# Cross attention: attention probabilities transposed by transfers of 16-bit halves instead of on TensorE

## The chip, the cores and the metric

The kernel runs on one core of one Trainium2 chip. A core has five engines that run side by side, each with its own instruction stream that it works through in order: TensorE (PE in the profile; its weight loads are PEld), VectorE (DVE), ScalarE (ACT), GpSimd (POOL) and SyncE (SP), which here issues nearly all transfers. 16 DMA engines move the data. The on-chip memory SBUF has 128 partitions; TensorE writes to a second memory, PSUM. The metric is the device time of one execution in microseconds (us), lower is better. The kernel before takes 880.24 us, the median of three runs (879.62 to 881.49).

## The reference

One layer of a perceiver in single precision. 16 batches; each has 64 latent rows `x` and a context of 512 rows, all of width 512. Three stages, each added to `x`: cross attention of the latents over context and latents, self attention with two softmaxes, and a gated feed-forward with weights and activations rounded to a 4-bit grid. The change lies in the first:

```
xn = _ln(x, g_x, b_x)                       # x: the context, (16, 512, 512)
ln = _ln(latents, g_l, b_l)                 # (16, 64, 512)
q = ln @ w_q
kv_in = jnp.concatenate([xn, ln], axis=1)   # 576 rows
k, v = jnp.split(kv_in @ w_kv, 2, axis=-1)  # 8 heads of 64
sim = jnp.einsum('bhid,bhjd->bhij', q, k)   # masked
attn = jax.nn.softmax(sim, axis=-1)
out = jnp.einsum('bhij,bhjd->bhid', attn, v)
return _ln(out.transpose(...) @ w_out, g_o, b_o)
```

So per batch and head there is a 64 x 576 matrix of probabilities. The product with `v` sums over the 576, and TensorE sums over partitions: the probabilities, which come out with the queries on the partitions, have to be transposed first.

## The kernel before

The program first works out the latents' queries, keys and values (`latents`), then the cross attention over the batches (`cross_attention`), into whose spare time on VectorE, ScalarE and GpSimd it lays the rounding of the feed-forward weights (`quant.tick()`), and then self attention and feed-forward. The order of instructions of every engine is the order of the program text; it is written out by hand, and `in_order` (L82) keeps it.

All large products are made three times (`Common.terms`, L114 to 126): both operands are split in a high and a low part, and high times high, low times high and high times low are summed, with four chunks of 128 each, so 12 matmuls of 512 columns for one product. The context comes twice: with its rows on the partitions (`nat`, 1 MB a batch, for mean and deviation, `Context.load` and `stats`) and transposed (`raw`, four chunks of 256 KB, `fetch`), which ScalarE casts to the high part (`Context.high`, L362) and VectorE or GpSimd subtracts from to get the low part (`Context.low`, L368).

The loop over the batches (L1152 and on) has in each batch b this order on TensorE, with what stands beside it:

- `keys(b, 0)`: a product for the keys of heads 0 and 1; VectorE scales it out of PSUM (L941). Then `turn(b - 1)` and `turn_latents(b - 1)`; in odd batches from 3 on also the transpose of an earlier output (`out_turn`, `ot`).
- `keys(b, 1)`, `keys(b, 2)`, `keys(b, 3)`, and between them ScalarE's casts of the next context and the loads of the one after.
- `scores(b, 0)` for the first pair of key chunks (four heads), `softmax(b, 0)`: VectorE takes the scores out of PSUM with the mask (L986), ScalarE takes the exponential (L990), into a tile `pr` of 2 x 576 columns, two buffers.
- `finish(b - 1)`: the product of the previous batch's probabilities with its values, first the latents' part (`weigh_latents`, L1039), then the context's (`weigh`, L1055), in the order r = 0 of pair 0, r = 0 of pair 1, r = 1 of pair 0, r = 1 of pair 1.
- `scores(b, 1)`, `softmax(b, 1)`.
- `values(b, 0)` to `values(b, 3)`: products for the values; ScalarE scales them out of PSUM (L954). In odd batches an output product (`po`) stands between the second and the third.
- At the end: ScalarE writes the next batch's mask (L913), SP issues the load of `nat` three batches on (`cx.load`, L314).

`turn` (L994) transposes the context's part of the probabilities of a batch: for two pairs `a`, two rows of heads `r`, four blocks `j` of 128 columns and two heads `c` one transpose of 64 x 128 on TensorE (L1004), 32 in all, into two PSUM tiles; ScalarE copies them to four tiles `prT` (L1013), which `weigh` uses as stationary operands. `turn_latents` (L1016) does the same with the 64 latent columns: two transposes, one copy to a tile `prl` (tag `two_h`, two buffers).

SP issues transfers one after the other; each first waits for the semaphore of its lane, of which there are eight, so at most eight are under way, and for the engines whose data or buffers it needs. What stands behind a waiting issue waits too.

Of the kernel before, what the change touches and what calls it, by code (L numbers as in the profile page):

```python
# [9 lines left out]
F32 = mybir.dt.float32  # L10
F32R = mybir.dt.float32r
U32 = mybir.dt.uint32
U8 = mybir.dt.uint8
AF = mybir.ActivationFunctionType
ALU = mybir.AluOpType
AX = mybir.AxisListType
# [3 lines left out]
P = 128  # L20
D = 512
KC = D // P
B = 16
S = 64
# [835 lines left out]
def cross_attention(tc, cm, sc, i, cw, cx, w1, w2, att, quant):  # L860
# [41 lines left out]
    def latents_values(b):  # L902
        if b >= B:
            return
        p, e = divmod(b, 2)
        vl = state[b]["vl"] = w2.tile([P, KC, S], F32, tag="two_l", bufs=2, name=f"vl_{b}")
        src = sc.v[p][e * S : (e + 1) * S].rearrange("p (n two d) -> p n two d", two=2, d=S)
        for h in range(2):
            nc.sync.dma_start(vl[h * S : (h + 1) * S], src[:, :, h, :])
# [22 lines left out]
    def keys(b, m):  # L932

        k = ends.pop((b, m))
        hi, lo = cx.done[b]
        cols = slice(m * P, (m + 1) * P)
        ps = cm.mm(f"pk_{b}_{m}")
        cm.product(
            ps, lambda c: (w_k[0][:, c, cols], w_k[1][:, c, cols], hi[:, c, :], lo[:, c, :]), range(KC)
        )  # L940
        nc.vector.tensor_tensor(k[:, S : S + N], ps, cx.row[b], ALU.mult)  # L941
        state[b]["k"].append(k)
# [31 lines left out]

    def softmax(b, a):
        st = state[b]
        st["pr", a] = w1.tile([P, 2, N + S], F32, tag="pr", bufs=2, name=f"pr_{b}_{a}")

        def two(t):
            return t.rearrange("p (h n) -> p h n", h=2)  # L980

        for r, ps in enumerate(st.pop(("sim", a))):
            mask = masks[b % 2][:, columns_of(r)[0]]
            pr = st["pr", a][:, r, :]
            least = cm.small.tile([P, 1], F32, tag="least", name=f"least_{b}_{a}_{r}")
            nc.vector.tensor_tensor_reduce(  # L986
                two(pr), ps[:, :, :half], two(mask), -1.0, BIG, ALU.add, ALU.min, least
            )
            t = 2 * a + r
            nc.scalar.activation(  # L990
                pr, pr, AF.Exp, bias=least, scale=-1.0, accum_out=st["tot"][:, t : t + 1]
            )

    def turn(b):  # L994

        pts = [cm.two(f"prt_{b}_{a}") for a in range(2)]
        for a, pt in enumerate(pts):
            for r in range(2):
                first = columns_of(r)[1].start
                for j in range(NJ):  # L1000
                    at = (r * NJ + j) * S
                    for c in range(2):
                        rows = slice(c * S, (c + 1) * S)
                        nc.tensor.transpose(  # L1004
                            pt[:, c, at : at + S],
                            state[b]["pr", a][rows, r, first + j * P : first + (j + 1) * P],
                            cm.ident[rows, rows],
                        )
        for a, pt in enumerate(pts):
            for r in range(2):  # L1010
                prT = w1.tile([P, NJ, P], F32, tag="prT", bufs=4, name=f"prT_{b}_{a}_{r}")
                src = pt[:, :, r * NJ * S : (r + 1) * NJ * S].rearrange("p c (j q) -> p c j q", q=S)
                nc.scalar.copy(prT.rearrange("p j (c q) -> p c j q", q=S), src)  # L1013
                state[b]["prT", a, r] = prT

    def turn_latents(b):  # L1016
        st = state[b]
        prl = w2.tile([P, 2, P], F32, tag="two_h", bufs=2, name=f"prl_{b}")
        pt = cm.ps_av.tile([P, D], F32, tag="av", name=f"prlt_{b}")[:, : 2 * P]
        pt = pt.rearrange("p (n q) -> p n q", q=P)  # L1020
        for a in range(2):
            pr = st.pop(("pr", a)).rearrange("p r t -> p (r t)")
            nc.tensor.transpose(pt[:, a, :], pr[:, N : N + P], cm.ident)
        nc.scalar.copy(prl, pt)
        st["prl"] = prl

    def weigh_latents(b):

# [123 lines left out]
    for b in range(B):  # L1152

        def tick():
            if b:
                quant.tick()

        done = (b - 3) // 2 if b >= 3 and b % 2 else None
        last = b == B - 1
        keys(b, 0)  # L1160
        if last:
            att.load("Wq")
            att.load("Wk")
        cx.high(b + 1, 0)
        if b >= 4 and b % 2 == 0:
            out_moments((b - 4) // 2)
        if b > 1:
            tick()
        if b:
            turn(b - 1)  # L1170
            turn_latents(b - 1)
        if done is not None:
            out_turn(done)
        keys(b, 1)
        cx.low(b + 1, 0)
        cx.high(b + 1, 1)
        if b > 1:
            tick()
        keys(b, 2)
        if done is not None:  # L1180
            out_low(done)
        cx.fetch(b + 2, 0)
        if b == 0:
            for k in range(KC):
                load_o(k)
        cx.flat(b + 1)
        cx.low(b + 1, 1)
        cx.high(b + 1, 2)
        tick()
        if last:  # L1190
            att.split("Wq", 0, 1)
        if b == 0:
            scores(b, 0)
            softmax(b, 0)
        keys(b, 3)
        cx.fetch(b + 2, 1)
        if b:
            scores(b, 0)
            softmax(b, 0)
        cx.low(b + 1, 2)  # L1200
        cx.high(b + 1, 3)
        if b:
            finish(b - 1)
            scores(b, 1)
            softmax(b, 1)
            around(b + 1, 2, 3)
            around(b + 2, 0, 1)
        tick()
        values(b, 0)
        cx.every(b + 1)  # L1210
        cx.low(b + 1, 3)
        cx.stats(b + 2, 0)
        tick()
        if last:
            att.split("Wq", 2, 3)
            att.load("Wv")
        if b == 0:
            scores(b, 1)
            softmax(b, 1)
            around(b + 1, 2, 3)  # L1220
            around(b + 2, 0, 1)
        values(b, 1)
        begin(b + 1)
        latents_values(b + 1)
        cx.fetch(b + 2, 2)
        cx.stats(b + 2, 1)
        tick()
        if last:
            att.norm(0)
            att.split("Wk", 0, 1)  # L1230
        tick()
        if done is not None:
            out_product(done)
        tick()
        values(b, 2)
        cx.fetch(b + 2, 3)
        cx.stats(b + 2, 2)
        tick()
        if done is not None:
            out_norm(done)  # L1240
            out_add(done)
        if b == 0:
            weight_o(0)
            weight_o(1)
        if b == 2:
            att.sa.load()
        if b == 5:
            att.sa.work()
        if last:
            att.split("Wk", 2, 3)  # L1250
            att.load("Wo")
            att.turn(0)
        values(b, 3)
        cx.stats(b + 2, 3)
        cx.spread(b + 2)
        mask(b + 1)
        if b == 0:
            weight_o(2)
            weight_o(3)
        quant.tick()  # L1260
        cx.load(b + 3)
    turn(B - 1)
# [42 lines left out]
class SelfAttention:  # L1305
# [42 lines left out]
    def turn(self, t):  # L1348
        cm, w2 = self.cm, self.w2
        pt = cm.ps_av.tile([P, D], F32, tag="av", name="zt_1") if t == 1 else cm.tr(f"zt_{t}")  # L1350
        cm.transpose_chunks(pt, self.st.pop(("z", t)), KC)
        zh = w2.tile([P, KC, P], F32R, tag="two_h", bufs=2, name=f"zh_{t}")
        zl = w2.tile([P, KC, P], F32R, tag="two_l", bufs=2, name=f"zl_{t}")
        cm.split(zh, zl, pt.rearrange("p (k n) -> p k n", n=P))
        self.st["zT", t] = zh, zl
# [299 lines left out]
class FeedForward:  # L1655
# [111 lines left out]
    def turn_h(self, s):  # L1767
        cm, w2 = self.cm, self.w2
        t, c = s
        n = CHUNKS[c][1]  # L1770
        nk = n // P
        pt = cm.tr(f"ht_{t}_{c}")
        cm.transpose_chunks(pt, self.st.pop(("h", s)), nk)
        hh = w2.tile([P, KC, P], F32R, tag="two_h", bufs=2, name=f"hh_{t}_{c}")[:, :nk, :]
        hl = w2.tile([P, KC, P], F32R, tag="two_l", bufs=2, name=f"hl_{t}_{c}")[:, :nk, :]
        src = pt[:, :n].rearrange("p (k n) -> p k n", n=P)
        if s == self.steps[-1]:
            for k in range(nk):
                cm.nc.scalar.copy(hh[:, k, :], src[:, k, :])
            cm.nc.vector.tensor_tensor(hl, src, f32(hh), ALU.subtract)  # L1780
        else:
            cm.split(hh, hl, src)
        self.st["hT", s] = hh, hl
# [171 lines left out]
```

## Time and profile before

| | |
|---|---|
| median of 3 runs | 880.24 us (879.62 to 881.49) |
| profiled execution | 881.33 us |
| span of its instructions | 879.5 us |
| TensorE busy | 871.7 us, 99% of the span |
| weight loads | 719.2 us, 82% |
| VectorE busy | 687.2 us, 78% |
| ScalarE busy | 398.8 us, 45% |
| GpSimd busy | 296.2 us, 34% |
| queue q1 (transfers of SP) | 80136 packets, 109.48 MB, 38.2% of 16 engines |
| granted TensorE clock | 1.0 throughout the cross attention |

The span is the time from the first to the last instruction of one profiled execution. "Busy" is the time in which at least one instruction of the engine ran. The chain of waits is followed back from the last instruction, at each step to what released it. A group of instructions is given by line, engine, operation, the tiles written and read, the shapes and the count, then busy us and mean ns of one, then the idle time of the engine just before them and who ended it. In a timeline x4 means four such instructions in a row, and the time is theirs together. The cross attention runs from about 92 to 560 us; batch 10 starts at 373.88, batch 11 at 401.98, batch 12 at 433.19.

### The profile page before, as it was taken

Reading aid. Unit: us, or ns where it says so; the run is one execution under the profiler, and the core shown is the slowest. Engines: PE = TensorE matmul, PEld = TensorE weight load, DVE = VectorE, ACT = ScalarE, POOL = GpSimd, SP = SyncE. Lnnn points to the kernel's source line nnn. Section 1 sums busy time; section 2 is a strip of 40 time slices with the busy share of each in tenths; the row PEclk is TensorE's granted clock in tenths of the full one; section 3 lists DMA queues with packets and bytes.
Section 4 is the critical chain, followed back from the end, with each engine's and each line's share of the span. In section 5 each row is a group of like instructions: output and inputs, shape, how many; then the busy total and the mean of one; then the engine's idle time right before and its main releaser. Section 6 shows DMA issues by size and latency. Waiting matters only on the chain.

```text
span 879.5 us, 17521 instructions
## 1 busy us (share of the span) xinstructions
PE 871.7 (99%) x6743; PEld 719.2 (82%) x6743; DVE 687.2 (78%) x1457; ACT 398.8 (45%) x787; POOL 296.2 (34%) x341
## 2 busy tenths in 40 slices
PE   8999999999999999999999999999999999999998
PEld 8988787878787888778878888888888888888887
DVE  7734457789788887787888867688998897888876
ACT  5654454544544535354445455554556233332221
POOL 2334234235353352353433622545543120111100
PEclk9999999999999999999999999999999999999999
DMA  8464554644655455435644362240008330000000
GB/s 277 167 233 169 167 163 142 201 143 141 192 164 160 138 174 168 136 111 178 183 134 149 121 198 64 82 192 1 1 3 320 136 144 13 13 13 13 13 12 25
DMA packets 80379, 111.12 MB, mean 126 GB/s; under 512 B 33176, under 2 KB 39080, under 8 KB 79016
## 3 DMA queue, kind: packets, MB, share of 16 engines
q1 hardware_dynamic: 80136, 109.48, 38.2%
q8 instruction: 53, 0.87, 0.4%
q0 software_dynamic: 160, 0.52, 0.2%
q14 instruction: 30, 0.25, 0.1%
HBM read 84.26 MB, written 25.72 MB: 125 GB/s over the span
## 4 chain that ended last, share of the span: by engine, by line
PE 93%; DVE 3%; DMA 2%; ACT 1%; POOL 1%; issue 1%; SPq 0%; ACTq 0%; DVEq 0%; POOLq 0%
PE pv L121 20%; PE pk L121 19%; PE gu L121 13%; PE dn L121 6%; PE sim L967 4%; PE av L1055 4%; PE Wv L121 3%; PE wo L121 3%; PE po L121 2%; PE Wq L121 2%; PE Wk L121 2%; PE prt L1004 2%; PE lq L121 2%; PE lk L121 2%; PE lv L121 1%; PE ht L171 1%
## 5 line engine op out<-in xcount | busy, mean ns | idle before, releaser
L121 PE MATMUL pv<-xvh,x 128*128 128x512 f32 x512 | 133.0, 394 | 0.0
L121 PE MATMUL pk<-x,xkh 128*128 128x512 f32 x512 | 128.2, 392 | 0.0
L121 PEld LDWEIGHTS pv<-xvh,x 128*128 128x128 f32 x512 | 94.8, 188 | 26.2 <-issue 7.0
L121 PEld LDWEIGHTS pk<-x,xkh 128*128 128x128 f32 x512 | 94.9, 188 | 19.5 <-issue 0.4
L990 ACT ACTIVATE pr<-pr,least 128x576 f32<-128x576 f32 x64 | 49.1, 769 | 59.7 <-DVE least L986 59.7
L941 DVE TENSOR_TENSOR k<-pk,row 128x512 f32<-128x512 f32 x64 | 43.2, 675 | 39.2 <-PE pk L121 39.0
L368 POOL TENSOR_TENSOR x<-raw,x 128x512 fp32r<-128x512 f32 x32 | 41.6, 1301 | 85.8 <-ACT x L362 80.5
L121 PE MATMUL pv<-xvl,x 128*128 128x512 f32 x256 | 68.7, 390 | 0.0
L121 PE MATMUL pk<-x,xkl 128*128 128x512 f32 x256 | 68.5, 389 | 0.0
L954 ACT ACTIVATE v<-pv,rs 128x512 f32<-128x512 f32 x64 | 43.2, 684 | 54.8 <-PE pv L121 54.3
L121 PE MATMUL gu<-uT,fx 128*128 128x512 f32 (+1 forms) x288 | 67.0, 377 | 0.2 <-DMA uT<-u_d 0.2
L121 PE MATMUL gu<-gT,fx 128*128 128x512 f32 (+1 forms) x288 | 65.8, 376 | 0.0
L121 PEld LDWEIGHTS gu<-gT,fx 128*128 128x128 f32 x288 | 52.2, 188 | 7.6 <-ACT fx L129 0.2
L121 PEld LDWEIGHTS gu<-uT,fx 128*128 128x128 f32 x288 | 51.8, 188 | 7.7 <-DMA uT<-u_d 0.5
L121 PEld LDWEIGHTS pv<-xvl,x 128*128 128x128 f32 x256 | 48.0, 188 | 10.3
L121 PEld LDWEIGHTS pk<-x,xkl 128*128 128x128 f32 x256 | 48.1, 188 | 10.2
L986 DVE CUSTOM_DVE_ANT_0 pr<-sim,mask 128x576 f32<-128x576 f32 x64 | 45.8, 753 | 5.3 <-PE sim L967 4.3
L205 ACT ACTIVATE qe_h<-qe_h,mmagic 128x512 f32<-128x512 f32 (+1 forms) x24 | 16.5, 687 | 66.7 <-DVE qe_h L202 64.6
L321 DVE BATCH_NORM_STATS2 cst<-nat 128x6 f32<-128x512 f32 x64 | 42.8, 669 | 3.7 <-DMA nat<-in_ctx_dram 3.7
L121 PE MATMUL dn<-dT,hh 128*128 128x512 f32 x170 | 42.9, 392 | 0.0
L967 PE MATMUL sim<-k,mask 64*64 64x288 f32 x512 | 40.4, 415 | 0.3 <-DMA mask<-q_d 0.3
L362 ACT CAST x<-raw 128x512 fp32r<-128x512 f32 x64 | 39.1, 631 | 0.0
(347 smaller groups left out, 1867.1 us busy)
## 6 DMA issues: line engine op xcount, KB each, us to landing
nat<-in_ctx_dram SPq DMA_DIRECT2D x16, 1024.0 KB
raw<-in_ctxT_dram SPq DMA_DIRECT2D x64, 256.0 KB
d_d<-qhl_d SPq DMA_DIRECT2D x11, 512.0 KB
row<-rs_d SPq DMA_DIRECT2D x16, 256.0 KB
g_d<-qhl_g SPq DMA_DIRECT2D x8, 512.0 KB
u_d<-qhl_u SPq DMA_DIRECT2D x8, 512.0 KB
gT<-g_d SPq DMA_DIRECT2D x4, 1024.0 KB
uT<-u_d SPq DMA_DIRECT2D x4, 1024.0 KB
```

The source lines that it names most:

```text
L121: self.nc.tensor.matmul(ps, lhsT=p[i], rhs=p[j], start=start and n == 0, stop=stop and n == last)
L205: nc.scalar.activation(e, e, AF.Relu, bias=self.mmagic, scale=MAGIC)
L321: nc.vector.bn_stats(st, self.nat[b][:, j, :])
L362: self.cm.nc.scalar.copy(self.done[b][0][:, c, :], self.raw[:, c, :])
L368: by.tensor_tensor(lo, self.raw[:, c, :], f32(hi), ALU.subtract)
L941: nc.vector.tensor_tensor(k[:, S : S + N], ps, cx.row[b], ALU.mult)
L954: nc.scalar.mul(v, ps, cx.rs[b][:, t : t + 1])
L967: nc.tensor.matmul(pss[r][c * S : (c + 1) * S, h, :half], lhsT=queries[b % 2][rows, m, :], rhs=st["k"][m][rows, at : at + half], start=Tru ...
L986: nc.vector.tensor_tensor_reduce(two(pr), ps[:, :, :half], two(mask), -1.0, BIG, ALU.add, ALU.min, least)
L990: nc.scalar.activation(pr, pr, AF.Exp, bias=least, scale=-1.0, accum_out=st["tot"][:, t : t + 1])
L1004: nc.tensor.transpose(pt[:, c, at : at + S], state[b]["pr", a][rows, r, first + j * P : first + (j + 1) * P], cm.ident[rows, rows],)
L1055: nc.tensor.matmul(st["av"][r][rows, a, :], lhsT=prT[:, j, rows], rhs=st["v"][j][:, at : at + S], start=False, stop=j == NJ - 1, skip_grou ...
```

## The change

For batches 0 to 14 the context's probabilities are no longer transposed by TensorE. Four bytes of a number are taken as two 16-bit halves:

- `halves(b, a)`: ScalarE copies the low and the high halves of a pair's probabilities into two 16-bit tiles of 2 x 512 columns (tag `two_h`, now three buffers). For pair 0 right behind the first value copy (in batch 0 behind the second), for pair 1 at the end of the batch, behind the fourth value copy and the mask.
- `send(b, a)`: SP issues for each half one transfer that transposes, 128 partitions x 1024 columns in blocks of 128 x 128, into a tile `far`, which takes a buffer of tag `pr`. For pair 0 behind the third value product, for pair 1 behind the first key product of the next batch.
- `join(b, a)`: ScalarE puts the two halves of each number together again and writes `prT`, two copies a pair. For pair 0 behind the second key product of the next batch, for pair 1 behind the third.

`turn_latents` stays on TensorE, but moves from behind the first key product of the next batch to behind the second value product of its own. Its target `prl` now shares a tile with the latents' values (`both`, tag `two_l`). The last batch keeps `turn` and `turn_latents` as they were. The tile of the probabilities is made 128 columns wider, so that a regular view `wide` reaches the context's columns of both rows.

```
@@ latents_values
-        vl = state[b]["vl"] = w2.tile([P, KC, S], F32, tag="two_l", bufs=2, name=f"vl_{b}")
+        both = w2.tile([P, 2, KC * S], F32, tag="two_l", bufs=2, name=f"lat_{b}")
+        vl = state[b]["vl"] = both[:, 0].rearrange("p (n d) -> p n d", d=S)
+        state[b]["prl"] = both[:, 1].rearrange("p (n q) -> p n q", q=P)
@@ softmax
-        st["pr", a] = w1.tile([P, 2, N + S], F32, tag="pr", bufs=2, name=f"pr_{b}_{a}")
+        wide = w1.tile([P, 2 * (N + 2 * S)], F32, tag="pr", bufs=2, name=f"pr_{b}_{a}")
+        st["wide", a] = wide.rearrange("p (r n) -> p r n", r=2)
+        st["pr", a] = wide[:, : 2 * (N + S)].rearrange("p (r n) -> p r n", r=2)
@@ new
+    def halves(b, a):
+        st = state[b]
+        src = st.pop(("wide", a))[:, :, :N].bitcast(U16).rearrange("p r (n h) -> p h r n", h=2)
+        for h in range(2):
+            half = w2.tile([P, 2, N], U16, tag="two_h", bufs=3, name=f"half_{b}_{a}_{h}")
+            nc.scalar.copy(half, src[:, h])
+            st["half", a, h] = half
+
+    def send(b, a):
+        st = state[b]
+        far = w1.tile([P, 2 * (N + 2 * S)], F32, tag="pr", bufs=2, name=f"far_{b}_{a}")
+        far = far[:, : 2 * N].bitcast(U16).rearrange("p (h n q) -> p h n q", h=2, q=P)
+        for h in range(2):
+            half = st.pop(("half", a, h)).rearrange("p r n -> p (r n)")
+            nc.sync.dma_start(far[:, h], half, transpose=True)
+        st["far", a] = far
+
+    def join(b, a):
+        far = state[b].pop(("far", a))
+        for r in range(2):
+            prT = w1.tile([P, NJ, P], F32, tag="prT", bufs=4, name=f"prT_{b}_{a}_{r}")
+            dst = prT.rearrange("p j q -> p (j q)").bitcast(U16).rearrange("p (n h) -> p n h", h=2)
+            src = far[:, :, r * NJ : (r + 1) * NJ].rearrange("p h j q -> p (j q) h")
+            nc.scalar.copy(dst, src)
+            state[b]["prT", a, r] = prT
@@ turn_latents
-        prl = w2.tile([P, 2, P], F32, tag="two_h", bufs=2, name=f"prl_{b}")
+        prl = st["prl"]
@@ the loop over the batches
         keys(b, 0)
+        if b:
+            send(b - 1, 1)
...
-        if b:
-            turn(b - 1)
-            turn_latents(b - 1)
...
         keys(b, 1)
+        if b:
+            join(b - 1, 0)
...
         keys(b, 2)
+        if b:
+            join(b - 1, 1)
...
         values(b, 0)
+        if b and not last:
+            halves(b, 0)
...
         values(b, 1)
+        if b == 0:
+            halves(b, 0)
+        if not last:
+            turn_latents(b)
...
         values(b, 2)
         cx.fetch(b + 2, 3)
+        if not last:
+            send(b, 0)
...
+        if not last:
+            halves(b, 1)
         quant.tick()
         cx.load(b + 3)
```

Outside the cross attention only the number of buffers of `two_h` changes from two to three, in `SelfAttention.turn` and `FeedForward.turn_h`.

## The prediction

> **What bounds the kernel now.** I read the page first, then the chain of waits over one batch of the cross attention, then ScalarE, the queue of SP and the DMA engines in that same batch. From the page, busy times and the chain that ended last:
>
> ```profile
> PE 871.7 (99%) x6743; PEld 719.2 (82%) x6743; DVE 687.2 (78%) x1457; ACT 398.8 (45%) x787; POOL 296.2 (34%) x341
> ...
> PE 93%; DVE 3%; DMA 2%; ACT 1%; POOL 1%; issue 1%; SPq 0%; ACTq 0%; DVEq 0%; POOLq 0%
> ```
>
> TensorE is the bound, and its instructions follow each other without gaps. So whatever is taken from it is gained, as long as nothing it waits for comes later than it comes now. The chain of waits in batch 11, which starts at 401.98 (start us, us, what):
>
> ```profile
> 401.98 2.72 PE pk L121 x12
> 404.69 1.14 PE prt L1004 x32
> 405.83 0.37 PE prlt L1023 x2
> 406.20 0.44 PE ot L171 x4
> 406.64 8.18 PE pk L121 x36
> 414.81 1.13 PE sim L967 x16
> 415.94 0.23 PE av L1039 x16
> 416.18 2.02 PE av L1055 x64
> ```
>
> The reader sees the price of `turn`: 32 transposes of probabilities, 1.14 us a batch. They lie right behind the first key product, and their results are used some 10 us later, by `av` L1055. Busy time by stage for an even and an odd batch (PE, PEld, DVE, ACT, POOL, clock, DMA share, GB/s), and for two microseconds inside the odd one:
>
> ```profile
> 373.88:401.98 28.10, 28.10 (x244) 22.51 (x243) 23.41 (x53) 13.77 (x28) 13.16 (x15) 1.00 0.49 144
> 401.98:433.19 31.21, 31.21 (x259) 25.19 (x259) 24.77 (x59) 14.55 (x31) 10.96 (x13) 1.00 0.51 161
> ...
> 406.00:408.00 2.00, 2.00 (x13) 1.75 (x12) 0.39 (x1) 1.54 (x4) 0.79 (x1) 1.00 0.94 349
> ```
>
> ScalarE and the DMA engines are half free, VectorE only a sixth. But at 406 to 408 the DMA engines are full: that is the 1 MB load of the next context (`nat`), issued as the timeline of SP shows (start, us, what):
>
> ```profile
> 403.15 0.38 SPq L314 DMA_DIRECT2D nat<-in_ctx_dram  x1
> ```
>
> **The change, part by part.** All times below, called T, count from the start of a batch.
>
> *Removed from TensorE:* `turn` of batches 0 to 14 (that of batch 15 stays): 15 x 1.14 = 17.1 us, all of it on the path.
>
> *Moved:* `turn_latents` (prlt, 0.37) goes from the next batch's start to behind the second value product. Same instructions, 0 us, but a nearer deadline: it needs the second pair's exponentials, which ended at 421.67 + 0.18, so T = 19.9, and with `turn` gone earlier at about 18.4. TensorE gets there at 10.9 + 0.44 + 1.13 + 0.23 + 2.02 + 1.13 + 5.4 = 21.3. Cover 2.9 us; 0 us.
>
> *ScalarE.* These groups give the prices (busy, mean ns), and the timeline shows that copies in a row overlap:
>
> ```profile
> L1013 ACT COPY prT<-prt 128x512 f32<-128x512 f32 x64 | 32.6, 594 | 0.0
> ...
> L1456 ACT ACTIVATE ex<-ex 128x1024 f32<-128x1024 f32 x8 | 8.5, 1062 | 22.6 <-DVE ex L1447 22.6
> ```
>
> ```profile
> 406.88 2.04 ACT L1013 COPY prT<-prt 128x512 f32<-128x512 f32 x4
> ```
>
> Four copies of 512 went, 0.51 each. Eight of 1024 elements come (four `halves`, four `join`); 1062 ns less the same overlap of some 0.1 is 0.96 each. Net 8 x 0.96 - 2.04 = 5.6 us a batch, so ScalarE is at 19.4 of about 27 in the even batch. The two copies behind the first value copy fit between it and the second (the product between them takes 2.72, the value copy 0.69, leaving 2.0 for 1.9). The join reads its two 16-bit parts alternately from places 2 KB apart; no row of this trace reads so. From below it costs as a plain copy, 0.96; from above twice that. I take the plain price, as no strided row here is dearer (the prT copies also rearrange), and keep the upper end as a rival.
>
> The Trainium skill (SBUF — State Buffer, the note on "cachelines") speaks against that price: accesses that change the 16-byte line each time pay a penalty, and the join's reads do. It gives no figure; no run here shows it yet.
>
> *The transfers.* Per batch four transposing transfers of 256 KB on the queue of SP. None is in this trace. One engine of 16 gets 64 pieces if a piece is a 256-byte source row. The trace's packets of 256 bytes took 17.8 ns on average, so t = 64 x 17.8 ns = 1.14 us a transfer. From above: if pieces were as small as what lands in one partition (16 values, 32 bytes), there would be 512 per engine at about 9.8 ns (packets of 4 bytes took 9.0, of 128 bytes 11.9), so t = 5.0 us. I take 1.14, since the source rows are 256 bytes and rows of that very size are in the trace.
>
> The rule in VectorE: DVE Perf Modes, "The three transpose paths", speaks against the whole change: it puts a 128x128 block at 1309 ns by transfer against 390 by TensorE. Eight blocks in a row at that price would be 10.5 us a transfer, and the four of a batch 42; with the 14 the engines have now that is 28 over the batch's 28, 15 x 28 = 420 us, some 1300 in all (estimates from that page). This trace shows TensorE's side far cheaper than 390 (1.14 us for 32 half blocks) and nothing of the other.
>
> *Does the second pair arrive in time?* The fourth value copy ends at T = 0.7 (402.70), the mask at 1.3, the two half copies at 2.3 and 3.25. SP can issue at 2.4 and 3.3. The `nat` load stands before them in the same queue; its packets end near T = 6.5 (408.5; the 256 KB behind it is issued later in the new order). So the transfers land at 6.5 + 2t + 0.4 = 9.2, the joins end at 10.1 and 11.1. TensorE comes to the weighing of that pair at 10.9 + 1.13 + 0.23 + 0.5 = 12.76, and to its second half at 13.76. Cover 2.6 us; it is gone at t = 2.45. The first pair has more than half a batch: no cost.
>
> *What stands behind the wait.* ScalarE comes to the second `join` at about T = 6.7 and waits 2.5 us. Behind it are a cast of the next context, the exponentials, and now and then a ScalarE step of the weight quantiser, on which VectorE waits in order, and VectorE frees the PSUM of the key products. Now such a step costs VectorE 0.3 us:
>
> ```profile
> L207 DVE SCALAR_TENSOR_TENSOR qw_g<-qe_g,qw_g 128x512 f32<-128x512 f32 (+1 forms) x12 | 8.2, 682 | 3.5 <-ACT qe_g L205 3.4
> ```
>
> From below 0 (VectorE has 28.10 - 23.41 = 4.7 us free); from above the whole 2.5 of each batch, 37 us. I take 0.5 us a batch, 7.5 us, nearer the lower end because VectorE uses the cast behind the wait only at 417.52 (T = 15.5, without `turn` about 14), after the joins have ended.
>
> *SP.* 60 more issues. An issue now takes 0.33 to 0.6 us; the longest single rows are 2.0 (with a wait in it). Four a batch: 1.5 to 8 us on a queue that is solid from 414.4 to 429.1 and then rests until 434.3. The first pair's two fall into that rest. At 0.6: 0 us. At 2.0 the second pair would land at 3.3 + 2 x 2.0 + 1 = 8.3 at the earliest, still below 9.2; the loads behind (the context's next chunk, issued at 410.73, T = 8.75) then have no rest left. So 0, and up to 1 us a batch above 2.0.
>
> *The rest:* three tiles in place of two for `two_h`, the latents' tile joined with `vl`, and `far` in the buffers of `pr`: `far` of pair 1 needs only its own half copies; the next batch's first exponentials' tile needs the joins that ended at 11.1, used at T = 13. Cover 2 us; 0. Batch 15 and all behind it are untouched.
>
> *Sum.* -17.1 + 7.5 = -9.6 us. The profiled execution took 881.33 (span 879.5 and 1.8 around it), 1.1 above the median: 881.3 - 9.6 = 871.7, and on the median 880.24 - 9.6 = 870.6. I say 871.
>
> **The rivals.**
>
> *Small pieces (slower).* If transfers move at the 32-byte price, the pair lands at 6.5 + 10 + 0.4 and the join ends at 17.9 instead of 12.76: 5.1 us late a batch, less 1.14. And the DMA engines have 20 us more beside their 0.5 x 28.1 = 14: 34 in a batch of 28, 6.5 over, 15 x 6.5 = 98 us: 979. It starts to cost at t = 2.45 and cancels the gain at 3.0. For it: no transposing row here. Against: whole 256-byte source rows. Its middle is 930.
>
> *The join at half speed (slower).* 1.82 instead of 0.96, 4 x 0.86 = 3.4 us a batch more. The joins end at 11.0 and 12.9, just in time, but ScalarE is at 23 of 27 and everything behind is late. None of it on TensorE: 871; all of it: 871 + 51 = 922. A third, since 3 us stay idle: 888. It decides above 0.65 us a batch.
>
> *SP runs out (slower or same).* Issues of 2.5 us and more delay `nat` and the context's chunks; 1 us a batch is lost: 886; at about 2 us the gain is just used up on VectorE's waits: 880.
>
> *Nothing new (hidden anyway)* is excluded for the removed part: TensorE does not wait there now.
>
> **How the numbers follow.** Forecast 0.45, with a range of its own from 863 (no wait at all) to 878. Small pieces 0.20, evenly from 880 to 980. Half-speed join 0.20. SP 0.15, half of it within 0.2%, which is about what a measurement of this kernel can tell from no change (1.8 us). Faster 0.45, same 0.08, slower 0.47. The range goes from 862 to 930, which leaves out half of the small pieces and little else.
>
> **What would show it.** No prt before batch 15; PE busy lower by 17 us; half and join copies near 1 us each (the rival: 1.8); ScalarE waiting for a transfer at the second join for about 2.5 us; av L1055's line without a wait for ScalarE; DMA share up from 0.5 to some 0.65 (0.9 and more if pieces are small); transposing issues on SP of 0.6 us (2 and more for that rival). The prediction is wrong if TensorE waits for the joins, and the size of that wait over 15 batches says by how much.

## The result, and the profile after

| | before | after |
|---|---|---|
| median | 880.2 us (879.62 to 881.49) | 886.66 us (886.17 to 887.05) |
| ratio after / before | | 1.0071 (95% interval 1.0054 to 1.0088) |
| profiled execution, span | 881.33, 879.5 | 886.17, 884.4 |

The change makes the kernel 0.7% slower; 871 was forecast, and faster. The time lies inside the range, on the other side of no change. The page of the kernel after, busy times and the chain that ended last:

```profile
PE 862.4 (98%) x6263; PEld 708.2 (80%) x6263; DVE 686.8 (78%) x1457; ACT 488.4 (55%) x847; POOL 294.7 (33%) x341
...
PE 67%; DMA 11%; DVE 11%; ACT 6%; SPq 3%; issue 2%; POOL 1%; DVEq 0%; ACTq 0%; POOLq 0%
```

TensorE's work fell, by 9.3 us in this row, not by the 17 that the prediction gives as its sign: the scores' busy time rose from 40.4 to 44.8 us and the weighing's from 33.4 to 37.0, some of it at the slow clock of the last section. And the chain, 93% TensorE before, is now only 67% TensorE: transfers and VectorE have taken a tenth each. The same from the start of batch 0 (at 81.76 before, ten us earlier than the start of the cross attention given above) to the start of batch 15, first before, then after (window, length, busy us of PE, PEld, DVE, ACT, POOL, then TensorE's clock, DMA share, GB/s):

```profile
81.76:520.42 438.66, 438.38 (x3613) 351.32 (x3612) 341.41 (x769) 209.34 (x421) 174.50 (x196) 1.00 0.51 157
```

```profile
81.79:525.86 444.07, 429.60 (x3167) 340.54 (x3166) 341.49 (x770) 295.57 (x480) 172.66 (x197) 0.99 0.72 187
```

The whole loss is in these 15 batches, 5.4 us. TensorE was idle for 0.3 us there and is now idle for 14.5; ScalarE has 86 us more, and the DMA engines went from half to 0.72 busy. Batch by batch (us from one first key product to the next):

| batch | 0 | 1 | 2 | 3 | 4 | 5 | 6 | 7 | 8 | 9 | 10 | 11 | 12 | 13 | 14 |
|---|---|---|---|---|---|---|---|---|---|---|---|---|---|---|---|
| before | 25.4 | 28.1 | 28.1 | 31.5 | 28.1 | 31.8 | 28.1 | 31.6 | 28.1 | 31.2 | 28.1 | 31.2 | 28.1 | 31.2 | 28.1 |
| after | 27.4 | 32.2 | 27.7 | 36.4 | 27.7 | 33.2 | 27.9 | 31.4 | 26.8 | 30.5 | 26.8 | 30.0 | 27.2 | 32.2 | 26.8 |

Batches 8, 10, 11 and 14 show the gain undisturbed: 1.30 us in an even batch and 1.25 in an odd one. Over 15 batches that is some 19 us. Batches 0, 1, 3, 5 and 13 are longer than before by 13.4 us together, more than the others gain (8.0). The waits of TensorE in the cross attention of the kernel after (waited for: us in total, times, longest):

```profile
PE av L1088 <- ACT prT L1047: 9.9, 5, 4.6
PE sim L970 <- DVE least L991: 2.3, 6, 0.6
PE prlt L1057 <- ACT pr L995: 2.0, 1, 2.0
```

The first row is the weighing of the second pair, which waits for the joins. The chain of waits in batch 3 says what the joins waited for (start us, us, what):

```profile
177.93 8.06 DMA far<-half
...
186.06 1.17 ACT prT L1047
187.23 0.04 issue
187.27 2.45 PE av L1088 x48
189.72 1.86 PE sim L970 x16
```

The second transposing transfer took 8.06 us from its issue to its landing. The timeline of SP there:

```profile
171.69 0.57 SPq L294 DMA_DIRECT2D g_d<-qhl_g  x1
...
175.90 0.38 SPq L315 DMA_DIRECT2D nat<-in_ctx_dram  x1
176.39 6.05 SPq L1037 DMA_TRANSPOSE far<-half  x2
```

Ahead of the pair stand a 512 KB store of the quantiser, some small loads and the 1 MB `nat`; the two issues alone hold SP for 6.05 us. The groups of copies on ScalarE and of the weighing on TensorE:

```profile
L1047 ACT COPY prT<-far 128x1024 uint16<-128x1024 uint16 x60 | 67.2, 1173 | 20.3 <-DMA far<-half 20.3
...
L1027 ACT COPY half<-pr 128x1024 uint16<-128x1024 uint16 x60 | 59.7, 1041 | 2.4 <-DMA far<-half 2.4
...
L1088 PE MATMUL av<-v,prT 128*64 128x64 f32 x1024 | 37.0, 231 | 10.0 <-ACT prT L1047 9.9
```

The copies cost little more than forecast. But ScalarE waits 20.3 us at the joins, and TensorE 9.9 us behind them. VectorE waits as well, for a cast that stands behind the joins on ScalarE:

```profile
DVE x L369 <- ACT x L363: 15.8, 5, 4.5
```

The two longest of these waits, 4.5 and 4.1 us, lie in batches 1 and 3, behind the late pair. The kernel before has no wait for this cast.

### The profile page after: what moved, and what is told of

It reads as the page before. It is cut to its first block, busy times and chain, and to the rows that moved or that the text cites. A ratio compares the mean times of both kernels' runs of the same rounds, so it can differ in the third digit from the quotient of the medians.

```text
span 884.4 us, 16760 instructions
## 1 busy us (share of the span) xinstructions
PE 862.4 (98%) x6263; PEld 708.2 (80%) x6263; DVE 686.8 (78%) x1457; ACT 488.4 (55%) x847; POOL 294.7 (33%) x341
## 4 chain that ended last, share of the span: by engine, by line
PE 67%; DMA 11%; DVE 11%; ACT 6%; SPq 3%; issue 2%; POOL 1%; DVEq 0%; ACTq 0%; POOLq 0%
PE gu L122 14%; PE pv L122 12%; PE pk L122 7%; PE dn L122 7%; DMA far<-half 4%; PE sim L970 3%; PE Wv L122 3%; PE wo L122 2%; PE Wq L122 2%; PE Wk L122 2%; PE po L122 2%; PE av L1088 2%; PE lq L122 2%; PE lk L122 2%; DMA g_d<-qhl_g 2%
## 5 line engine op out<-in xcount | busy, mean ns | idle before, releaser
L122 PE MATMUL pv<-xvh,x 128*128 128x512 f32 x512 | 135.1, 395 | 0.0
L122 PEld LDWEIGHTS pv<-xvh,x 128*128 128x128 f32 x512 | 94.2, 188 | 25.7 <-issue 7.2
L1047 ACT COPY prT<-far 128x1024 uint16<-128x1024 uint16 x60 | 67.2, 1173 | 20.3 <-DMA far<-half 20.3
L1027 ACT COPY half<-pr 128x1024 uint16<-128x1024 uint16 x60 | 59.7, 1041 | 2.4 <-DMA far<-half 2.4
L122 PEld LDWEIGHTS pv<-xvl,x 128*128 128x128 f32 x256 | 48.0, 188 | 10.5
L206 ACT ACTIVATE qe_h<-qe_h,mmagic 128x512 f32<-128x512 f32 (+1 forms) x24 | 16.5, 687 | 66.4 <-DVE qe_h L203 64.3
L970 PE MATMUL sim<-k,mask 64*64 64x288 f32 x512 | 44.8, 429 | 2.3 <-DVE least L991 2.3
L1088 PE MATMUL av<-v,prT 128*64 128x64 f32 x1024 | 37.0, 231 | 10.0 <-ACT prT L1047 9.9
```

The costliest lines, as they stand in the source:

```text
L122: self.nc.tensor.matmul(ps, lhsT=p[i], rhs=p[j], start=start and n == 0, stop=stop and n == last)
L206: nc.scalar.activation(e, e, AF.Relu, bias=self.mmagic, scale=MAGIC)
L970: nc.tensor.matmul(pss[r][c * S : (c + 1) * S, h, :half], lhsT=queries[b % 2][rows, m, :], rhs=st["k"][m][rows, at : at + half], start=Tru ...
L1027: nc.scalar.copy(half, src[:, h])
L1047: nc.scalar.copy(dst, src)
L1088: nc.tensor.matmul(st["av"][r][rows, a, :], lhsT=prT[:, j, rows], rhs=st["v"][j][:, at : at + S], start=False, stop=j == NJ - 1, skip_grou ...
```

## The experiments

Theory A: the second pair comes late because of what stands ahead of it on SP's queue. Theory B: ScalarE's eight copies a batch, in order with everything else there, are the price. Theory C: the transposing issues hold up SP, and what is behind them is late.

**Without the transfers (e2).** In `send` and `join`:

```
-            nc.sync.dma_start(far[:, h], half, transpose=True)
+            (left out; join reads the probabilities where they lie)
```

> The changed kernel without its 60 transposing transfers: the joins read the probabilities where they lie (untransposed, so the output is another), the halves are still copied and thrown away. ScalarE's eight copies a batch stay, SP's issues and the transfers go. Theory A (late arrival): all of the gain shows, 15 x 1.3 us as in the undisturbed batches: 880.2 - 19.5 = 861, no wait of TensorE over 1 us. Theory B (ScalarE's work): 880 to 887 as before. Theory C: as A, 861; A and C are told apart by the other runs.

Measured: 872.32 us (871.15 to 872.74), ratio 0.9913 (0.9897 to 0.993). So the transfers cost 14.3 us of the 886.7. But it is not 861: some 11 us go in another way, to which e13 to e17 return. Batch 7 shows where (chain of waits; it starts at 282.34):

```profile
296.56 0.68 DVE k L944
297.24 0.67 DVE pr L992
...
297.96 1.87 PE sim L970 x16
```

VectorE comes late to the keys and the scores, and the second scores on TensorE (1.13 us undisturbed) follow at its pace.

**Without the load ahead (e9).**

```
+        if 3 <= b < B:
+            self.nat[b] = self.kept          # context 2's tile, no transfer
```

> The changed kernel (886.7 us) without the 1 MB load of nat for contexts 3 to 15 (13 MB of the queue; their statistics are taken from context 2, so the output is another). All transposing transfers, their issues, the stores and all copies stay. Theory A (the second pair is late because of what stands ahead of it on the one queue): only the 512 KB store is left ahead, the pair lands before T = 9.5 in every batch, TensorE's waits for the joins go, and the kernel comes to the level of e2, 871 to 875. Theory C (the transposing transfers themselves, 1.24 us and more of SP each and 1.6 us of the engines): they are all still there, 884 to 888.

875.23 us (874.43 to 877.72), ratio 0.9942 (0.9926 to 0.9957). The 60 transposing transfers and their issues are still there; with the 13 loads out of their way 11.4 of the 14.3 us come back. TensorE's wait for the joins:

```profile
PE av L1091 <- ACT prT L1050: 1.2, 3, 0.6
```

From 9.9 us to 1.2. A shorter wait of VectorE for `nat` itself is not the reason: it is 3.4 us in the kernel after, and 4.3 here. So theory A holds, and the transfers and their issues alone (theory C) cost no more than the rest of some 3 us.

**The pair first, the load behind it (e1).**

```
             send(b - 1, 1)
+            cx.load(b + 2)
...
-        cx.load(b + 3)
```

> The 1 MB load of the next context (nat) is issued behind the second pair's two transposing transfers, not ahead of them; nothing else differs from the changed kernel (886.7 us). Theory A (the second pair arrives late because nat, and in odd batches a 512 KB store of the quantiser too, stand ahead of it in the one queue): the second pair lands some 3 us earlier, the waits of TensorE for the joins (3.68, 4.65, 0.92, 0.49 us in batches 1, 3, 13, 5) shrink to a fifth at most, and with them the slow clock behind the two long ones (2 us each): 886.7 - 8 - 4 = 875, and 868 if the small waits of VectorE go as well. Theory B (ScalarE's eight copies a batch are the price, in order with the casts and exponentials): the copies are all still there, 884 to 888. Theory C (SP is held up by each transposing issue, 1.24 us and more, and what is behind comes late): the issues are all still there, and nat now comes behind them: 885 to 892.

901.42 us (900.89 to 902.0), ratio 1.0242 (1.0227 to 1.0258): slower than any theory had it. What A said of the pair came true: the odd batches from 3 to 11 took 29.96 us, and the wait for the joins went to 2.4 us. But the even batches took up to 37.8. Their chain of waits, in batch 4:

```profile
216.04 7.17 DMA u_d<-qhl_u
...
223.31 0.10 DVE qhl_u L288
...
225.33 2.86 PE sim L970 x16
228.19 7.45 PE pv L122 x24
```

The quantiser's store now stands behind `nat`. VectorE refills the store's buffer, so it waits for its landing, and the scores wait for VectorE (20.1 us in all). The wait had been moved, not removed. A part of the 901 is the slow clock behind these waits: the mean granted clock was 0.985, against 0.996 in the kernel after, which is some 10 us of clock time over the span (an estimate from these two numbers). The run also shows an undisturbed transposing transfer, in a window in which only the pair moves:

```profile
460.40:463.10 2.70, 2.70 (x14) 2.23 (x13) 2.63 (x6) 2.52 (x3) 2.36 (x5) 1.00 1.01 191
```

All DMA engines are busy, at 191 GB/s: 256 KB in 1.37 us.

**The load behind the store too (e5), and batch 0's latents later (e6).** e5 puts `cx.load(b + 2)` ahead of `keys(b, 2)`; e6 moves `turn_latents(0)` behind `values(0, 2)` besides.

> As e1_send_first (901.4 us), but the load of nat goes one step further back, behind the quantiser's 512 KB store that follows the two transfers. In e1 the joins were on time and VectorE waited instead for that store, whose buffer it refills (TensorE waited 20.1 us for VectorE, and the even batches lost 36 us against the undisturbed 26.8). Theory A2 (what hurts is only which item stands behind the 1 MB load; an order exists in which nobody waits): the store lands some 3 us earlier, these 36 us go, and the kernel comes to 865 to 872. Theory D (the queue of SP is simply too long in each batch now, and the last in it is late whatever the order): the wait moves to the statistics of nat or to the casts of the context, 880 to 900.

> As e5_load_after_store, and in batch 0 alone the transposes of the latents' probabilities (prlt) go behind the third value product. In the changed kernel TensorE waits 2.0 us for them there, since batch 0 computes its second scores later than the other batches. Expected 2 us less than e5, 3 if the clock falls in that gap; no difference if the wait is taken up by the next one.

e5: 887.37 us (884.99 to 888.83), ratio 1.0072 (1.0054 to 1.0089). e6: 886.8 (885.85 to 890.15), 1.0074 (1.0054 to 1.0095). Neither differs from the changed kernel: theory D. In e5 the waits are spread over `sim` (5.9 us), `prlt` (2.3), `av` (1.9) and `pk` (1.9). In e6 batch 0 took 25.7 in place of 29.9 us, and batch 1 took 34.2 in place of 28.2.

**The load on another queue (e4).**

```
-            self.cm.nc.sync.dma_start(self.nat[b], ...
+            by = self.cm.nc.scalar if b >= 3 else self.cm.nc.sync
+            by.dma_start(self.nat[b], ...
```

> The changed kernel, with nat of contexts 3 and later issued on ScalarE's queue instead of SP's, at the same place of the program. nat no longer stands ahead of the second pair in its queue, but moves at the same time over the same 16 engines. Theory A (order on the queue): the second pair lands 2 to 3 us earlier, 870 to 878. If what counts is the engines' bytes (1 MB moving at that time) and not the order, the pair is as late as now: 884 to 888. Theory B: 886 or more, since ScalarE also issues. Theory C (SP held up): the issues fall back to 1.24 us, and the kernel to some 870.

889.75 us (888.59 to 890.68), ratio 1.0109 (1.0094 to 1.0124): the order on SP's queue is not the whole of it. By the records of the packets, the pair's began only when most of `nat`'s had moved in the odd batches (batch 5: `nat`'s from T = 5.6 to 9.7, the pair's from 9.0; batch 1: 9.6 to 15.8, and 13.1), with a second issue of 2.7 to 5.5 us; in the even batches from 4 to 12 they began earlier but lasted until T = 10.6 to 13.0, where without `nat` beside them (e1, batches 6 to 12) they end at 7.2 to 8.3. In the odd batches from 3 on a store still goes ahead of the pair on SP's own queue; batch 1 has none there and is late all the same. So theory A has to be put more widely: the bytes ahead of the pair and beside it on the DMA engines make it late, on whichever queue they are.

**The first pair alone by transfer (e3), and with e6's move (e8).**

```
+            turn(b - 1, (1,))      # 16 transposes, second pair
-            send(b - 1, 1); join(b - 1, 1); halves(b, 1)
```

> Only the first pair of each batch goes by transfer; the second is turned by TensorE as before the change (16 transposes a batch). Theory A (only the second pair is late): half the gain and no new wait, 15 x 0.6 = 9 us: 871 (869 to 873). Theory B (ScalarE): half the added copies, 883. Theory C (SP's issues): half the issues, 882 to 885.

> As e3_first_pair_only (884.0 us), with prlt of batch 0 behind the third value product as in e6. e3's even batches took 27.65 us and its undisturbed odd ones 30.75, 0.45 less each than before the change; it lost 2.1 us in batch 0 and some 6 in batches 3, 5, 7 and 13. With the first loss gone: 881.5 to 882, no difference from before. If the others go too (they follow from batch 0's delay): 876 to 878.

e3: 884.04 us (883.52 to 887.05), ratio 1.0052 (1.0033 to 1.0071); e8: 885.8 (885.14 to 887.01), 1.0058 (1.0043 to 1.0073). Here no pair is late, TensorE never waits for a join in e3, and still nothing is gained. A's 871 is wrong. The undisturbed batches gain 0.44 us, but batch 0 loses 2.1, and batches 5, 7 and 13 lose 1.2, 0.8 and 2.3. The chain of waits in batch 13 of e3:

```profile
465.26 3.95 DMA d_d<-qhl_d
...
469.30 0.72 DVE qhl_d L288
...
472.73 2.12 ACT prT L1047 x2
474.85 0.52 ACT x L363
475.36 0.63 ACT qe_d L206
476.02 1.26 DVE qw_d L208
```

It goes through the quantiser: its store, for whose landing VectorE waits 1.3 us, its transpose on VectorE, then ScalarE, where the joins stand ahead of its next step (L206), for which VectorE had waited 2.0 us; behind that on VectorE come the keys and the scores. In the kernel before, the chain of this batch is TensorE alone from end to end.

**Without the halves (e13, e14).** e13 is e2 with e6's move, e14 leaves out the half copies besides.

> As e2_no_transfers (872.3 us; no transfers, joins read the untransposed probabilities, output not the reference's), with prlt of batch 0 behind the third value product. In e2 batch 0 took 29.5 us, 4.1 more than before the change and 5.4 more than it could; without transfers the queue is as before, so nothing should take up the wait: 872.3 - 4 to 5 = 867 to 868. If the delay comes back in batches 1 to 3 as it did from e3 to e8 and from e5 to e6, it is not the transfers that make it: 871 to 872.

> As e13, without the four half copies a batch as well (the joins, which read the probabilities themselves, stay). If ScalarE's added time delays the batches with the quantiser's 512-wide pieces (3, 5, 7, 13; 0.8 to 1.7 us each in e2), half of the addition gone should leave half of that: 3 us less than e13, 864 to 865. If it is the joins alone, because they lie between the quantiser's step on ScalarE and VectorE's use of it: as e13.

e13: 872.72 us (871.1 to 873.93), ratio 0.9908 (0.9894 to 0.9922); e14: 870.01 (868.03 to 872.24), 0.9879 (0.986 to 0.9898). What batch 0 wins by the move (29.5 to 25.2) batches 1 to 3 mostly lose (85.3 to 88.7), the second case of e13's expectation. The half copies, some half of ScalarE's added time, are worth 2.7 us, near the 3 that e14's first case gives for them; but the two ranges overlap, and in e14, too, batches 3, 5, 7 and 13 are 1.6 to 2.7 us above the 29.96 us of an undisturbed odd batch.

**The first pair's joins on GpSimd (e7), or earlier (e15).** e7 is e6 with `nc.gpsimd.tensor_copy` for these joins. e15 is the changed kernel with `join(b - 1, 0)` right behind `send(b - 1, 1)`, ahead of the casts and the quantiser's step.

> As e6, and the joins of the first pair (two copies of 1024 16-bit values a batch, 1.17 us each on ScalarE) are made by GpSimd, which is a third busy. Without transfers the changed kernel was at 872 and not at the 861 of the removed work (e2), and the missing us were put down to ScalarE's longer order in the batches of the quantiser. If that is right: 3 to 6 us less than e6. If it is VectorE's own order: as e6 within 1 us. If GpSimd's copies of this shape are slow (over 3 us each) or hold up its quantiser steps: slower than e6.

> The changed kernel (886.7 us) with the first pair's joins right behind the issue of the second pair's transfers, before the casts of the context and the quantiser's step, in place of behind the second key product. The first pair has long landed there. If VectorE's waits for the quantiser's step on ScalarE, which stands behind these joins, are what costs in batches 3, 5, 7 and 13 beside the late arrival: ScalarE's rest of 1.6 to 1.9 us before the quantiser's cast takes the joins, and each of these four batches is 1 to 1.5 us shorter: 881 to 883. If the late second pair alone counts: 885 to 888.

e7: 891.51 us (891.14 to 892.62), ratio 1.0124 (1.0107 to 1.0141). GpSimd's copy took 1221 ns, hardly more than ScalarE's; ScalarE now waits 17.2 us at the second pair's joins, where it waited 4.7 in e6. Why this is 4.7 us slower than e6 was not followed up. e15: 885.23 (881.88 to 890.34), 1.0072 (1.0043 to 1.0102): as slow as the changed kernel. VectorE's waits for the quantiser's step did fall, from 15.4 to 10.7 us, but those for the cast L363 rose from 15.8 to 20.9. Batch 7 took 29.96 us in place of 31.43; that is no gain, since batch 6 before it took 30.50 in place of 27.89. (Batch 7 is as short with the joins in their old place, after a long batch 6, in e1, e4 and e11.) TensorE's longest waits are those for the late pair and for batch 0's latents:

```profile
PE av L1088 <- ACT prT L1047: 10.1, 5, 5.3
PE prlt L1057 <- ACT pr L995: 2.8, 1, 2.8
```

**The change in some batches only (e10, e11, e12, e16, e17).** The other batches keep `turn`:

```
+    FAR = range(5, 12)            # e10; e12: (1, 3, 5, 7, 8, 9, 10, 11, 13)
-        if b:
+        if b - 1 in FAR:
             send(b - 1, 1)
...
+        if b and b - 1 not in FAR:
+            turn(b - 1)
+            turn_latents(b - 1)
```

e11 is e10 with the load as in e5; e16 is e10 with the early joins of e15; e17 is e16 with `range(5, 14)`.

> The change in batches 5 to 11 alone (transfers, halves and joins in the order of the changed kernel); batches 0 to 4 and 12 to 15 are turned by TensorE as before. From the changed kernel's own batches: 7 to 12 took 0.14, 1.31, 0.75, 1.31, 1.25 and 0.92 us less than before the change, 6 took 0.20 less: 5.9 in sum, 880.4 - 5.9 = 874.5. If the gain in these batches was only time taken back from a delay of the earlier ones: 879 to 881.

> As e10_some_batches, with the load of nat in these batches behind the second pair's transfers and the quantiser's store, as in e5 and e6. From e6's rows the batches 6 to 12 gain 1.17, -0.09, 1.32, 1.25, 0.92, 0.55 and 1.31, 6.4 us in sum: 874. If theory D holds here too (the wait only moves along the queue): as e10 within 1 us.

> The change in batches 1, 3, 5, 7, 8, 9, 10, 11 and 13 alone; the others are turned by TensorE. The second pair of an odd batch has no quantiser's store ahead of it in the next batch and came in time in the changed kernel (batches 2, 4, 6 took 0.39, 0.40 and 0.20 less than before the change although batches 1 and 3 had been late, 8 to 12 and 14 between 0.75 and 1.31). Theory A: each of the periods 2, 4, 6, 8 to 12 and 14 gains 0.4 to 1.3, in sum 8 to 10: 870 to 873. If the early odd batches bring nothing because SP is still late there: 874 to 876, as e10.

> As e10_some_batches (876.4 us, the change in batches 5 to 11), with the early joins of e15. In e10 batch 7 took 31.67 and not 30.0 us; the others were at their best. If the place of the joins is the reason: 1 to 1.6 us less, 875. If not: 876 to 877.

> As e16, with the change in batches 5 to 13. Batch 14 then gains 1.3 us, and batch 13 loses 0.4 to 1 as in the changed kernel if its joins are late, and gains 1.2 if the early place cures it: 873 to 875.

| | us | ratio to before |
|---|---|---|
| e10 | 876.36 (873.67 to 876.83) | 0.9951 (0.9936 to 0.9965) |
| e11 | 875.94 (874.34 to 876.83) | 0.9949 (0.9937 to 0.9962) |
| e12 | 876.03 (875.02 to 877.89) | 0.9949 (0.9935 to 0.9963) |
| e16 | 875.12 (873.92 to 876.09) | 0.9949 (0.9937 to 0.9962) |
| e17 | 873.58 (872.34 to 875.45) | 0.9935 (0.9922 to 0.9949) |

All five beat both kernels. In e10, e11, e16 and e17 the crowded first batches are left as they were, and the later ones keep most of their gain; e12, which also takes early odd batches, missed its 870 to 873: batches 3, 5, 9 and 13 took 32.5, 32.5, 31.9 and 32.3 us, longer than before the change. e11 is as e10: moving the load brought nothing here either. The early joins are not seen to help: e16's range overlaps e10's, and batches 5 to 7 took 90.8 us in e16 and 90.6 in e10. In e17 batch 13 took 30.66 us against 32.17 in the changed kernel, with the pair still by transfer. TensorE's waits for VectorE and for the joins in e17:

```profile
PE sim L970 <- DVE least L991: 1.2, 2, 0.9
...
PE av L1088 <- ACT prT L1047: 0.3, 1, 0.3
```

## Why the prediction was wrong

**The step that failed** is the arrival: "its packets end near T = 6.5 [...] So the transfers land at 6.5 + 2t + 0.4 = 9.2, the joins end at 10.1 and 11.1", with 2.6 us of cover in every batch. It was read from one batch of the kernel before. In even batches it came true: `nat` ended at 5.8 to 7.0, the joins at 10.3 to 11.5 (13.6 in batch 2). In the odd ones from 3 on a store of 384 or 512 KB goes out ahead of `nat`, batches 1 and 3 have other loads of their own ahead, and `nat` itself is issued later than before (2.1 in place of 1.2 in batch 11): there `nat` ended at about 8 to 13 and the joins at 14.0 to 19.1, where TensorE comes to this pair's halves at 13.3 and 14.2 if nothing holds it up (batch 11). It waited for the joins in batches 1, 3, 5, 9 and 13, 3.7 and 4.6 us in the first two. "Cover 2.6 us" was true of half the batches. Taking the transfers out is worth 14.3 us (e2), taking `nat` out 11.4 (e9).

Step by step:

- *`turn` removed, 17.1 us:* too small. It is 1.30 a batch in batch 8 (1.14 for `prt`, the rest in `prlt` and the product behind it), some 19 in sum.
- *`turn_latents` moved, 0 us:* wrong in batch 0, whose second scores come after the first value product; TensorE waited 2.0 us. The cover was read in batch 11. Undoing it there did not pay: batches 1 to 3 gave it back (e5 to e6, e2 to e13).
- *ScalarE's copies at 0.96:* 1.04 and 1.17 for one, 1.00 and 1.12 by busy time. ScalarE's 86 us more are 5.7 a batch; 5.6 was forecast. The join at half speed (1.82) did not happen. The join takes 0.13 us more than the half copy; whether that is the alternate reading, no run separates.
- *Transfers of 1.14 us:* 1.37 (e1). 61440 packets of 256 bytes came, 1024 for each of 60 transfers, so the pieces are whole rows and the rival of small pieces falls. The 10.5 us worked out from the Trainium skill (VectorE: DVE Perf Modes, "The three transpose paths") falls too: eight blocks took 1.37 us.
- *SP, 0.6 us an issue, 0 us in sum:* a transposing issue takes 1.24 us at least and up to 4.5 when a large transfer is ahead; the first of the pair's comes at T = 3.4 at the earliest, not 2.4. The rival that SP runs out named part of what happened, but priced it by the issue. What counts is what is under way ahead of the pair: the DMA engines are 0.72 busy on average, and in batch 3 the pair's packets began at T = 12.5, with `nat`'s ending at 13.0, though the first was issued at 7.2.
- *VectorE behind the joins, 7.5 us:* the cast that VectorE was to use "after the joins have ended" came late where the joins did (waits of 4.5 and 4.1 us in batches 1 and 3). But time is lost without any late join as well. Without transfers (e2) the gain is 7.6 of some 19 us, so some 11 were lost: 4.1 in batch 0, slow clock included, about 6 in batches 3, 5, 7 and 13, the odd ones whose quantiser pieces are all 512 wide, and 1.0 in batch 4. (Batch 0 holds no `turn` and had nothing to gain, so the 5.4 in e13's expectation is 1.3 too much.) In batch 7 VectorE has little to spare: the kernel before had it busy for 26.98 of 31.57 us, and e2's chain there goes through it. Why it is late there stays open. ScalarE's longer order is likely: VectorE's waits for the quantiser's step rose from 10.1 us before to 16.7 in e2, and leaving out the half copies gave 2.7. But moving the first pair's joins ahead of that step gave nothing that these runs can tell from none (e15, e16).
- *Not foreseen:* a slow clock behind each long gap, below.

The sum without the late arrival, 870.6, lies near the 872.3 of e2, but by luck: the removed work was some 2 us more than its 17.1, the moved latents cost 4.1 in batch 0 where 0 was put, and the 7.5 stood for waits behind a second join that waits for its transfer, which e2 does not have; some 7 us were lost there in another way.

## What to carry to other kernels

Read the arrival of a new transfer in every kind of batch, not in one: what stands ahead of it in the queue differs with parity, with the first batches, and with the change itself. When a queue and the engines behind it are full at the moment that matters, a reordering moves the wait to whoever needs the last item; either bytes go, or the change is made only where there is room. Work that is moved off the bounding engine pays only as far as the next in-order engine has slack in that very batch. And read a gain over several batches: what one wins the next may lose, as batches 0 and 1 in e6 and 6 and 7 in e15.

## What the runs showed of the hardware

**TensorE's clock falls after a gap.** In batch 1 of the kernel after TensorE waits 3.68 us, until 125.93. Windows behind it (clock is the third figure from the right):

```profile
126.00:128.00 2.00, 2.00 (x44) 2.00 (x46) 0.51 (x1) 2.00 (x3) 0.00 (x0) 0.58 0.45 147
128.00:130.00 2.00, 2.00 (x26) 1.08 (x22) 1.25 (x6) 1.50 (x5) 0.43 (x1) 0.56 0.07 14
130.00:132.00 2.00, 2.00 (x12) 1.53 (x9) 1.70 (x5) 0.83 (x3) 0.85 (x1) 1.00 0.04 8
```

For 4 us it runs at little more than half speed: the 48 weighing products took 2.54 us, where 64 took 2.02 in the kernel before, so 48 some 1.5. The two long gaps (batches 1 and 3) cost 1.0 and 0.9 us more in the weighing and 0.7 each in the scores behind it, so a wait of 4 us is really one of 5 or more. The Trainium skill (TensorE: Matmul & The Clock Gate, "The HAM clock gate") has half rate after an idle window of about 3.4 us, free-running. The two gaps over 3.4 us agree. Shorter ones go both ways: after 2.00 us in batch 0 of the kernel after the clock stayed at 1.00, after 1.93 us in the same place of e2 it fell, and there the measurement decides:

```profile
101.58:103.58 2.00, 0.33 (x2) 0.00 (x0) 1.97 (x7) 1.42 (x3) 0.00 (x0) 1.00 0.97 330
103.58:105.58 2.00, 1.74 (x6) 1.38 (x7) 1.57 (x5) 2.00 (x5) 0.00 (x0) 0.65 0.32 120
105.58:107.58 2.00, 2.00 (x6) 1.62 (x5) 0.00 (x0) 0.93 (x2) 0.00 (x0) 0.50 0.39 111
```

There batch 0 took 29.5 us, and 27.4 in the kernel after, so a gap of 2 us may cost its own length again.

**A transposing transfer within SBUF moves little more than half of what a load does in the same time:** 191 GB/s with all engines busy, against 349 GB/s for `nat` at 0.94 in the kernel before. The skill (Advanced Engine Details and Errata, "X-Bar Transpose (TRN2)") has it as fast as a regular one, at 350 to 400; the measurement decides. And a large load delays its packets even from another queue (e4).
